# Loading each slab of left with two transfers of 64 x 8 pieces in place of four of 64 x 4

## The chip, the core and the metric

The kernel runs on one core of a Trainium2 chip. The metric is the device time of the whole program in microseconds (us), the median of several runs. Five engines matter: PE (matrix multiplies; PEld is its weight load), DVE, ACT and POOL (elementwise work) and SP, which does no arithmetic here and issues nearly all DMA transfers, one after the other, in the order of the program. SPq in the profile is SP's stream of such issues.

## What is computed

Two layers of the same form, one after the other, on x of 1 x 512 x 512 x 64 (f32). The reference, cut to what matters:

```python
for layer in (L0, L1):
    g = group_norm(x, groups=32)                      # over all rows and columns
    xn = layernorm(g, norm_scale, norm_bias)
    left  = (xn @ Wl + bl) * mask * sigmoid(xn @ Wlg + blg)
    right = (xn @ Wr + br) * mask * sigmoid(xn @ Wrg + brg)
    out = 0
    for dd in range(-4, 5):                           # a band of nine rows
        out += left[:, i + dd, i, None, :] * right[:, i + dd]
    out = layernorm(out) * sigmoid(xn @ Wog + bog)
    x = x + out @ Wo + bo
```

For each of 128 channels the band is a matrix of 512 x 512 that is zero but near its diagonal; it multiplies the rows of right.

## The kernel before

**Tiling.** The 512 rows are cut into 9 blocks of 64 rows that overlap (`row_blocks`), because one multiply takes a 64 x 64 piece of the band. The columns are taken in two halves at a time, one on partitions 0 to 63 and the other on 64 to 127; each half is cut into 4 chunks of 64 columns. A layer so has 36 chunks, and a chunk is one period of a schedule written out by hand as a table of steps (`FIRST`, lines 39 to 67, for the first layer, `SECOND`, lines 69 to 97, for the second). The loop of lines 1116 to 1119 walks through the table once a period and calls the step's function with a unit number (a unit is 8 columns of both halves, so a period has 8 units). Instructions go to each engine's queue in exactly this order.

**Tiles.** `z` is a unit's input (12 buffers), which POOL and DVE normalise and PE transposes into `ZT` and `zT`. PE multiplies these by the weights, ACT takes the sigmoid `sg`, and DVE writes right into `RO`. `A` holds the band of left for the block at hand: for each of 8 slabs h (16 channels), 8 pairs of channels, 64 columns of the band, on 64 partitions, and the same once more on the other 64 partitions. `mix` (line 710) multiplies a slab of `A` by `RO`, 64 multiplies for a slab, 8 slabs a chunk, and ACT or DVE copies the result back into `RO`. POOL and ACT then normalise `RO` into `on`, PE transposes `on`, DVE multiplies by the gate into `ZH`, PE multiplies by Wo, and DVE adds the old x, held in `XR` (6 buffers), which SP stores to `mid_x` in the first layer and to `out` in the second.

**Left.** Left is computed once a layer and written to `left_of` in DRAM in a spread form, in which a row of 2 x 64 f32 at the right offset is a row of the band (`spread_left`). `take_left` (line 696) reads slab h of block n from there into `A[:, h]`: four transfers, over the two halves of the partitions (e) and the two halves of the slab's channel pairs (k). Each moves 64 rows of 4 pieces of 512 B, 128 KB.

**When left is read.** After the copy of slab h in a block's last chunk, `on_copy` puts (next block, h) in the list `slabs` (line 1092). Each `load` step (`on_load`, line 967) first takes one entry from that list, issues its transfers with `take_left`, and then issues the two transfers of the next unit's `z`. So the eight slabs of the next block are read within about one period, one ahead of each pair of `z` transfers, on SP's one queue, between the `XR` transfers (`fetch`, line 866) and the stores (`stored`, line 899). For the first block of a layer the list is filled by line 938 in the same way. There are 9 blocks x 8 slabs x 2 layers = 144 slabs, and 576 transfers of left.

Of the kernel before, what the change touches and what calls it, by code (L numbers as in the profile page):

```python
# [20 lines left out]
WIN = 4  # L21
NEAR = 2 * WIN + 1
S = 64
# [4 lines left out]
HA = 16  # L28
# [129 lines left out]
def tile_two_banded_layers(  # L158
# [8 lines left out]
    H = layers[0]["Wl"].shape[1]  # L167
# [19 lines left out]
    span = 2 * (S + 2 * WIN)  # L187
    size = S * H // 2 * span
    left_of = dram.tile([2, size], F32, name="left_of")
# [86 lines left out]
    def strided(v: bass.AP, at: int, *dims) -> bass.AP:  # L276

        return bass.AP(tensor=v.tensor, offset=v.offset + at, ap=[list(d) for d in dims])
# [417 lines left out]
    def take_left(n: int, h: int):  # L696

        held[h] = n
        q = HA // 4
        for e in range(2):  # L700
            for k in range(2):
                en.sync.dma_start(
                    A[e * S : (e + 1) * S, h, k * q : (k + 1) * q].rearrange("p h i t -> p h (i t)"),
                    strided(
                        left_of, n % 2 * size + (h * HA // 2 + k * q) * span + 2 * WIN,
                        (H // 2 * span, S), (span, q), (1, 2 * S),
                    ),
                )

    def mix(c: int, h: int, b: str) -> tuple:  # L710

# [203 lines left out]
    def layer(src: bass.AP, dst: bass.AP, w: dict, stats: bool, then=None):  # L915
# [51 lines left out]
        def on_load(n, t, alt, b):  # L967
            if slabs:
                take_left(*slabs.pop(0))
            if t in units and t not in early:  # L970
                load(src, units[t])
# [106 lines left out]
        def on_band(n, t, alt, b):  # L1078
            if chunk(t):
                c, h = chunk(t)  # L1080
                while held.get(h) != c // per:
                    take_left(*slabs.pop(0))
                mixed[t] = mix(c, h, b)
# [141 lines left out]
    A = keep.tile([P, H // HA, HA // 2, S, 2], F32, name="A")  # L1225
# [63 lines left out]
```

## Time and profile before

| | |
|---|---|
| median of 3 runs | 4260.02 us (4246.09 to 4260.52) |
| the profiled execution's own span | 4279.5 us |
| busy: PE, DVE, POOL, ACT | 3741.4, 3681.0, 3584.7, 3320.3 us |
| transfers of left (`A<-left_of`) | 576 of 128 KB, all issued by SP |
| transfers of z, of XR, and stores | 1152 of 128 KB, 1152, 1152 (112 or 120 KB) |
| moved in all | 596.25 MB, mean 139 GB/s |

The profile is of a single execution, 19.5 us longer than the median. Durations and sums below are of that execution. In the timeline views a row has a start in us, a length in us (a merged row's length holds the small gaps in it), engine, line, operation, tiles and count, and in brackets the idle time before it with what ended it. In the view of stretches of time a row has the stretch, its length, the busy time of PE, PEld, DVE, ACT and POOL with counts, the granted clock of PE, the mean busy share of the 16 DMA engines, and GB/s. Nearly every instruction has line 491, which is the helper that records them, so they are told apart by tiles.

### The profile page before, as it was taken

To read this page: it belongs to the slowest core of one execution; us is meant where nothing else is said; L and a number is where in the kernel's file an instruction comes from. 1 tells how busy PE (TensorE), PEld (TensorE's weight loads), DVE (VectorE), ACT (ScalarE), POOL (GpSimd) and SP (SyncE) were. 2 spreads that over 40 slices of the span, in tenths; PEclk is the share of its full clock that TensorE was granted. 3 is DMA by queue.
4 is the path that set the end of the run, shared out by engine and by line. 5 is a ranking of instruction groups with operands and counts; after the bars stand their busy time and mean duration, and the time that the engine had idled before them with its cause. 6 is when DMAs were issued, how large, how long until landed. Compare 5 with 4: busy or idle time off the path is not lost.

```text
span 4279.5 us, 223070 instructions
## 1 busy us (share of the span) xinstructions
PE 3741.4 (87%) x94986; PEld 3208.3 (75%) x94986; DVE 3681.0 (86%) x9911; ACT 3320.3 (78%) x6372; POOL 3584.7 (84%) x4566
## 2 busy tenths in 40 slices
PE   0158999999999999999975889999999898989998
PEld 0057888888888888888864778787878787878786
DVE  8968888888888888888867889898989898989897
ACT  0047888888888888888863778888889788978887
POOL 2368999999999999999837789898989898989883
PEclk9989999999999999999997999999999999999999
DMA  9843545454545454545344354545454545444533
GB/s 396 321 102 96 150 112 152 117 147 114 152 115 151 116 152 117 153 115 155 104 119 114 98 141 120 145 120 148 121 147 119 146 116 145 123 142 122 149 105 96
DMA packets 695718, 596.25 MB, mean 139 GB/s; under 512 B 138310, under 2 KB 549990, under 8 KB 692420
## 3 DMA queue, kind: packets, MB, share of 16 engines
q1 hardware_dynamic: 692212, 580.43, 47.6%
q8 instruction: 748, 12.26, 1.2%
q14 instruction: 246, 2.02, 0.2%
q0 software_dynamic: 2512, 1.56, 0.1%
HBM read 436.71 MB, written 149.74 MB: 137 GB/s over the span
## 4 chain that ended last, share of the span: by engine, by line
PE 77%; issue 4%; POOL 3%; DVE 3%; SPq 2%; DMA 2%; ACT 2%; POOLq 0%; DVEq 0%; ACTq 0%
PE banks L491 59%; PE bank L491 14%; PE acc L491 4%; POOL z L491 3%; SPq L491 2%; DMA z<-mid_x 1%; POOL on L491 1%; DVE ZH L491 1%; DVE sto L491 1%; DVE RO L491 1%; ACT RO L491 0%; DVE z L491 0%; ACT on L491 0%; DVE XR L491 0%; ACT sg L491 0%
## 5 line engine op out<-in xcount | busy, mean ns | idle before, releaser
L491 ACT ACTIVATE on<-RO,nm,rs 128x128 f32<-128x128 f32 x2484 | 1144.3, 499 | 176.0 <-PE banks L491 150.4
L491 POOL TENSOR_SCALAR on<-RO,rs,nm 128x128 f32<-128x128 f32 x2124 | 958.6, 463 | 354.7 <-PE banks L491 308.4
L491 PE MATMUL banks<-pack,ZT 64*128 64x128 f32 x9216 | 1000.4, 287 | 28.5 <-DVE RO L491 13.9
L491 PE MATMUL banks<-pack,zT 64*128 64x128 f32 x9216 | 947.0, 277 | 3.7 <-issue 3.7
L491 DVE TENSOR_TENSOR RO<-banks,sg 128x512 f32<-128x512 f32 x1152 | 778.3, 684 | 181.9 <-ACT sg L491 158.6
L491 PEld LDWEIGHTS banks<-pack,ZT 64*128 64x128 f32 x9216 | 765.2, 191 | 152.9 <-ACT zT L491 35.6
L491 DVE BATCH_NORM_STATS2 sto<-RO 128x6 f32<-128x256 f32 x2304 | 852.5, 412 | 3.0 <-ACT RO L491 3.0
L491 DVE SCALAR_TENSOR_TENSOR ZH<-banks,pack,ZH 128x896 f32<-128x896 f32 (+1 forms) x576 | 667.4, 1159 | 198.2 <-PE banks L491 153.4
L491 ACT ACTIVATE sg<-banks 128x512 f32<-128x512 f32 x1170 | 691.6, 595 | 171.7 <-PE banks L491 133.0
L491 POOL TENSOR_TENSOR z<-z,ga 128x512 f32<-128x512 f32 x556 | 719.2, 1294 | 111.3 <-DMA z<-mid_x 91.0
L491 PE MATMUL banks<-RO,A 64*64 64x64 f32 x36864 | 699.4, 223 | 122.7 <-issue 117.5
L491 PEld LDWEIGHTS banks<-RO,A 64*64 64x64 f32 x36864 | 623.3, 136 | 222.8 <-issue 160.3
L491 PEld LDWEIGHTS banks<-pack,zT 64*128 64x128 f32 x9216 | 747.9, 192 | 5.0 <-issue 4.1
L491 POOL TENSOR_TENSOR z<-z,gb 128x512 f32<-128x512 f32 x556 | 717.8, 1291 | 3.5
L491 PE MATMUL bank<-pack,ZH 128*64 128x64 f32 x18432 | 666.3, 226 | 21.1 <-DVE ZH L491 11.2
L491 PEld LDWEIGHTS bank<-pack,ZH 128*64 128x64 f32 x18432 | 593.2, 139 | 111.3 <-issue 56.0
L491 ACT COPY RO<-banks 128x1024 f32<-128x1024 f32 x540 | 542.8, 1011 | 163.3 <-PE banks L491 154.1
L491 POOL TENSOR_TENSOR z<-z,rs 128x512 f32<-128x512 f32 x586 | 617.2, 1060 | 50.7 <-DVE rs L491 48.7
L491 POOL TENSOR_TENSOR z<-z,sti 128x512 f32<-128x512 f32 x586 | 621.9, 1071 | 35.8 <-DVE sti L491 31.8
L491 ACT ACTIVATE ZH<-banks 128x896 f32<-128x896 f32 (+1 forms) x576 | 535.4, 929 | 83.1 <-PE bank L491 55.4
L491 PE MATMUL banks<-ZT,pack 64*128 64x448 f32 (+1 forms) x2304 | 573.3, 572 | 2.6 <-DVE ZH L491 1.4
L491 DVE BATCH_NORM_STATS2 sti<-z 128x6 f32<-128x128 f32 x2344 | 509.4, 282 | 63.8 <-POOL z L491 62.9
(202 smaller groups left out, 4053.8 us busy)
## 6 DMA issues: line engine op xcount, KB each, us to landing
z<-in_x_dram SPq DMA_DIRECT2D x576, 128.0 KB
A<-left_of SPq DMA_DIRECT2D x576, 128.0 KB
z<-mid_x SPq DMA_DIRECT2D x576, 128.0 KB
gn_x<-in_x_dram SPq DMA_DIRECT2D x16, 4096.0 KB
XR<-in_x_dram SPq DMA_DIRECT2D x448, 112.0 KB
mid_x<-XR SPq DMA_DIRECT2D x448, 112.0 KB
XR<-mid_x SPq DMA_DIRECT2D x448, 112.0 KB
out_dram<-XR SPq DMA_DIRECT2D x448, 112.0 KB
```

What stands on the lines that cost most here:

```text
L491: return lambda *a, **k: tc.keep_in_program_order(f(*a, **k))
```

## The change

`take_left` no longer halves a slab's channel pairs: the loop over k goes, and each of the two transfers left moves 64 rows of 8 pieces, 256 KB. The bytes, the tiles and the order of everything else stay.

```diff
         held[h] = n
-        q = HA // 4
+        q = HA // 2
         for e in range(2):
-            for k in range(2):
-                en.sync.dma_start(
-                    A[e * S : (e + 1) * S, h, k * q : (k + 1) * q].rearrange("p h i t -> p h (i t)"),
-                    strided(
-                        left_of, n % 2 * size + (h * HA // 2 + k * q) * span + 2 * WIN,
-                        (H // 2 * span, S), (span, q), (1, 2 * S),
-                    ),
-                )
+            en.sync.dma_start(
+                A[e * S : (e + 1) * S, h].rearrange("p h i t -> p h (i t)"),
+                strided(
+                    left_of, n % 2 * size + h * q * span + 2 * WIN,
+                    (H // 2 * span, S), (span, q), (1, 2 * S),
+                ),
+            )
```

On SP's queue, at the last chunk of a block in the second layer, where the slabs of the next block are read, this stands before the change (x4 means four such transfers in a row):

```order
L491 DMA out_dram<-XR_1084 56x512 x2
L491 DMA A<-left_of 64x4x128 x4
L491 DMA z<-mid_x 64x512 x2
L491 DMA XR_1088<-mid_x 56x512 x2
L491 DMA XR_1087<-mid_x 56x512 x2
L491 DMA A<-left_of 64x4x128 x4
L491 DMA z<-mid_x 64x512 x2
```

and this after it:

```order
L491 DMA out_dram<-XR_1084 56x512 x2
L491 DMA A<-left_of 64x8x128 x2
L491 DMA z<-mid_x 64x512 x2
L491 DMA XR_1088<-mid_x 56x512 x2
L491 DMA XR_1087<-mid_x 56x512 x2
L491 DMA A<-left_of 64x8x128 x2
L491 DMA z<-mid_x 64x512 x2
```

Nothing has changed its place; each group of four transfers of left, ahead of a pair of z transfers, has become a group of two. At the start of the second layer, where the first block's slabs are read right behind the transfer that saves left (`left_rows`), SP's queue had

```order
L491 DMA left_rows<-A 128x4608
L491 DMA A<-left_of 64x4x128 x4
L491 DMA z<-mid_x 64x512 x2
L491 DMA A<-left_of 64x4x128 x4
L491 DMA z<-mid_x 64x512 x2
```

and has now

```order
L491 DMA left_rows<-A 128x4608
L491 DMA A<-left_of 64x8x128 x2
L491 DMA z<-mid_x 64x512 x2
L491 DMA A<-left_of 64x8x128 x2
L491 DMA z<-mid_x 64x512 x2
```

The first layer starts in the same manner. On PE, DVE, ACT and POOL the instructions and their order are the same before and after; only PE's multiplies of a new slab wait for two transfers where they waited for four.

## The prediction

> **What bounds the kernel now.** I read the page first. It shows that no single engine is full, and that PE carries most of the chain that ended last:
>
> ```profile
> span 4279.5 us, 223070 instructions
> PE 3741.4 (87%) x94986; PEld 3208.3 (75%) x94986; DVE 3681.0 (86%) x9911; ACT 3320.3 (78%) x6372; POOL 3584.7 (84%) x4566
> PE 77%; issue 4%; POOL 3%; DVE 3%; SPq 2%; DMA 2%; ACT 2%; POOLq 0%; DVEq 0%; ACTq 0%
> ```
>
> SPq has 2% and DMA 2% of the chain, some 170 us together. A share of the whole says little, so the next view is by stage. A period begins with PE's first multiply of a chunk's first slab; this one begins at 2915.50, the next at 2973.38, so this period is 57.9 us long:
>
> ```profile
> 2915.50 0.29 PE L491 MATMUL banks<-RO,A 64*64 64x64 f32 x4
> 2973.38 0.33 PE L491 MATMUL banks<-RO,A 64*64 64x64 f32 x5
> ```
>
> It is the last chunk of a block in the second layer, in which the next block's eight slabs are read. The view of stretches has all eight such periods of that layer (one of them and the sum), and then eight ordinary periods (one, and the sum):
>
> ```profile
> 2915.50:2973.40 57.90, 52.42 (x1263) 44.36 (x1259) 47.47 (x126) 45.78 (x91) 48.44 (x61) 0.94 0.67 186
> sum 487.20, PE 419.53 PEld 358.91 DVE 380.01 ACT 367.32 POOL 387.55; mean PE 52.44 PEld 44.86 DVE 47.50 ACT 45.92 POOL 48.44
> ...
> 2863.70:2915.50 51.80, 49.03 (x1259) 41.86 (x1256) 47.22 (x126) 45.46 (x91) 48.44 (x61) 1.00 0.38 101
> sum 409.10, PE 389.94 PEld 334.07 DVE 377.93 ACT 364.28 POOL 387.52; mean PE 48.74 PEld 41.76 DVE 47.24 ACT 45.54 POOL 48.44
> ```
>
> A reading period takes 487.2 / 8 = 60.9 us, an ordinary one 409.1 / 8 = 51.1 us, with the same counts and the same busy time on POOL, DVE and ACT. **The eight periods are 78.1 us too long in all, 9.8 us each.** PE's extra 30 us of busy time there come with a granted clock of 0.94 in place of 1.00, so they look like a consequence of PE having stood still, not a cause. What does it wait for? The chain of that one period, and who waited for whom from 2484.7 to 4048.5 us (the whole stretch that holds the eight):
>
> ```profile
> by line: PE banks L491 48.0%; SPq L491 18.3%; PE bank L491 14.4%; DMA z<-mid_x 11.3%; POOL z L491 4.4%; issue 2.2%; POOL on L491 1.5%; POOLq L491 0.1%
> ...
> POOL z L491 <- DMA z<-mid_x: 70.3, 16, 7.7
> PE banks L491 <- POOL on L491: 52.5, 15, 7.6
> ...
> 2924.70 1.27 POOL L491 TENSOR_TENSOR z<-z,ga 128x512 f32<-128x512 f32 x1 [3.26 <-DMA z<-mid_x]
> 3387.36 1.26 POOL L491 TENSOR_TENSOR z<-z,ga 128x512 f32<-128x512 f32 x1 [7.72 <-DMA z<-mid_x]
> ```
>
> POOL waits 16 times, two times in each reading period, for a z that has not landed, 70.3 us in all; its normalisations (`on`) stand behind that in its queue, and PE waits for them. The z is late because it was issued late. SP's queue in that period:
>
> ```profile
> 2906.85 0.76 SPq L491 DMA_DIRECT2D out_dram<-XR  x2
> 2916.70 3.51 SPq L491 DMA_DIRECT2D A<-left_of  x4
> 2920.33 1.18 SPq L491 DMA_DIRECT2D z<-mid_x  x2
> ...
> 2932.71 2.63 SPq L491 DMA_DIRECT2D A<-left_of  x4
> ...
> 2946.24 3.16 SPq L491 DMA_DIRECT2D A<-left_of  x4
> 2949.51 1.19 SPq L491 DMA_DIRECT2D z<-mid_x  x2
> 2950.75 2.58 SPq L491 DMA_DIRECT2D A<-left_of  x4
> 2953.44 1.20 SPq L491 DMA_DIRECT2D z<-mid_x  x2
> 2954.68 3.25 SPq L491 DMA_DIRECT2D A<-left_of  x4
> 2958.03 1.19 SPq L491 DMA_DIRECT2D z<-mid_x  x2
> ...
> 2973.86 1.87 SPq L491 DMA_DIRECT2D XR<-mid_x  x4
> 2977.04 1.20 SPq L491 DMA_DIRECT2D out_dram<-XR  x3
> ```
>
> From 2907.6 to 2916.7 it stands still, since the first slab may not be overwritten before PE has used it for the last time (2915.50). From 2916.7 to 2975.7, 59 us, row follows on row: **the queue is full, and sets the pace of the period.** The DMA engines behind it are busy only 0.67 of the time.
>
> **The change part by part.**
>
> *Issues.* Each reading period loses 16 of 32 issues of left. The price of one before, and of the nearest shapes:
>
> ```profile
> L491 SPq DMA_DIRECT2D A<-left_of x576: 573/613/2137, 261.6 to 4039.1; - x192
> L491 SPq DMA_DIRECT2D left_of<-left_rows x64: 550/586/1846, 363.8 to 3966.3; - x64
> L491 SPq DMA_DIRECT2D XR<-in_x_dram x576: 315/429/1902, 327.8 to 2226.1; - x192
> L491 SPq DMA_DIRECT2D XR<-mid_x x576: 306/391/1773, 2370.9 to 4263.9; - x192
> ```
>
> The middle number is the median: 613 ns. Four in the row at 2932.71 take 2.63 us, 657 ns each with the gap. What an issue of 64 x 8 pieces costs no row shows. Below stands 573 ns, the least of the 64 x 4 form; above 2 x 613 = 1226 ns, if the price went by pieces. The other rows speak for the low end: XR in the first layer is 56 x 4 pieces and in the second 56 x 1, and costs 429 against 391, 38 ns for three more pieces a row; a transfer of left_rows has 16 x 64 = 1024 pieces and costs 586, less than one of left with 256. I take 0.66 us, 0.70 with the gap. A slab then takes 1.41 us of the queue in place of 2.63, **1.22 us less, 9.8 us in eight slabs**; at 1226 ns it would be 0.1 us, nothing.
>
> *DMA engines.* The same bytes are now asked for in half the time, and the engines may take over as the limit. Their pace when they are full shows where the layers begin (share 1.11 and 1.03):
>
> ```profile
> 270.00:282.00 12.00, 8.23 (x88) 7.85 (x88) 8.43 (x28) 4.79 (x9) 11.92 (x11) 0.64 1.11 209
> 2302.00:2308.00 6.00, 2.97 (x52) 2.67 (x48) 5.72 (x18) 3.14 (x7) 5.92 (x6) 0.98 1.03 238
> ```
>
> A slab is 524 KB: 2.51 us at 209 GB/s, 2.20 at 238. If the engines set the pace in every slab, it saves 0.12 to 0.43 us, 1.0 to 3.4 us a period, not 9.8. Over a whole period they are not the limit: 0.67 x 57.9 = 39 us of work stand against 59 - 9.8 = 49 us of queue, a share of 0.79. But slabs stand close together (three between 2946 and 2958), and there the queue asks for more than they give. I take **7.5 us a period**, nearer to the queue's 9.8, because of the 0.79.
>
> *Where the stalls go.* The lateness at the end of a period is 9.8 us; 7.5 of it goes and 2.3 stay, most of it at the first z, which has one slab ahead of it alone (2916.70 to 2920.33) and can gain little over 1 us of its 3.26. The engines are late next, then the first wait of SP for PE, which the change doesn't touch. Eight periods: 8 x 7.5 = **60 us**. POOL's stall is on PE's path one to one within the reading: 70.3 us waited, 78.1 us too long.
>
> *First layer.* Its eight reading periods, and eight others:
>
> ```profile
> sum 429.80, PE 413.12 PEld 360.51 DVE 371.17 ACT 365.86 POOL 397.29; mean PE 51.64 PEld 45.06 DVE 46.40 ACT 45.73 POOL 49.66
> ...
> sum 432.60, PE 412.89 PEld 360.20 DVE 371.34 ACT 366.27 POOL 396.91; mean PE 51.61 PEld 45.02 DVE 46.42 ACT 45.78 POOL 49.61
> ```
>
> They are no longer than the others (53.7 against 54.1 us), with PE at 51.6: PE hides SP's late issues there. Gain nothing, and if that cover were thin the gain would be positive too.
>
> *Starts of the layers.* Here the queue is full as well, but so are the engines (share 0.99), just behind the save of left:
>
> ```profile
> 262.00:295.00 33.00, 24.57 (x296) 23.02 (x294) 23.99 (x79) 16.97 (x32) 24.91 (x22) 0.70 0.99 242
> ```
>
> Between 0 and 7 slabs x 1.22 = 8.5 us for each; with full engines I take 1 us each, **2 us**.
>
> *PE.* Its multiplies of a slab wait for two transfers in place of four. The slab is used a period after it is asked for (first asked at 2916.70, first used at 2973.38), so a longer transfer costs nothing; that cover is some 50 us thick.
>
> Sum: 60 + 2 = 62 us less than the profiled 4279.5, that is 4217.5; the runs shown have a median 19.5 us lower, and the same 62 us off 4260.0 give **4198 us**.
>
> **A rule against it.** The row first: in the page's reading above, SP issues left at 657 ns for 131 KB, 200 GB/s, and the engines behind it have time left. The Trainium skill, "DMA: Bandwidth & Descriptors", section "Issuing engines are not separate DMA queues", holds that the time to initiate a transfer is usually small beside the transfer itself. By that rule the engines set the pace, and the change would bring the 1.0 to 3.4 us a period of the second rival alone. The share of 0.67 in a period full of issues speaks against the rule here; the shares of 1.03 to 1.11 at the layers' starts speak for it there.
>
> **The rivals.**
>
> *All of it goes* (chance 0.19). The engines keep up, the longer issues that now and then come in a row of four (3.51 and 3.22 beside 2.63) become fewer too, and a reading period becomes an ordinary one: 78 us, with 3 us at each start 84, 4176 us. For it: 0.79 is below 1. Against: the first z of each period stays behind a slab.
>
> *The engines take over* (0.13). Each slab moves at 209 to 238 GB/s; 8 x 1.0 to 8 x 3.4 = 8 to 27 us, 4252 to 4233 us. For it: the rates of the full stretches. Against: they were taken with the save of left in the same queue.
>
> *The change doesn't do what it says* (0.07). The price goes by pieces, 1226 ns for twice as many, and SP's queue stays as full: 4260 us. Against: 1024 pieces for 586 ns.
>
> *Slower* (0.03). A transfer of left that stands before engines with work waiting blocks SP, and with twice the bytes it blocks longer. Such blocking is in the trace, at the start of the second layer:
>
> ```profile
> 2295.42 4.96 SPq L491 DMA_DIRECT2D A<-left_of  x4
> ```
>
> Four issues take 4.96 us there, against 2.63. The place is each reading period of the second layer; the point from which it decides is a pair that takes over 2.63 us, so engines that give less than 524 / 2.63 = 199 GB/s to left. At 175 GB/s a pair takes 3.0 us, 0.37 more, times 64 slabs: 24 us, 4284. Against: the lowest rate of full engines is 209.
>
> **How the numbers follow.** The forecast itself has 0.58, between 4180 and 4220. The range reaches from the full relief, 4176, to inside the engines' case, 4240. A measurement of this kernel can tell about 0.5%, 21 us, from no change. Faster by more: 0.58 + 0.19 + 0.09 of the engines' 0.13 = 0.86; within: 0.07 + 0.04 = 0.11; slower: 0.03.
>
> **What would show it.** In the changed kernel's profile: 288 issues of left with a median near 0.65 us (over 1.2 would mean the rival of the price); SP's queue with gaps again before the end of a reading period; POOL's waits for z from the second layer down from 70.3 us to 20 or less, the second wait of each period gone and the first left; reading periods of 53 to 54 us; a DMA share there near 0.75, and near 1 if the engines took over; PE's clock at 1.00 in most of them; the first layer as it is. It would be wrong if z lands later behind the longer transfers than it was issued earlier, which would show as the same waits of POOL with earlier issues.

## The result, and the profile after

| | before | after |
|---|---|---|
| median (lowest to highest) | 4256.42 us (4246.09 to 4260.52), 4 runs | 4206.19 us (4204.93 to 4215.75), 4 runs |
| span of the profiled execution | 4279.5 us | 4214.0 us |

After divided by before is 0.9882, 95% interval 0.9865 to 0.9899: 1.2% faster, 50 us by the medians. The profiled execution of before is 23 us longer than its median, that of after 8 us, so the profiles differ by 65 us; what follows takes stages from the profiles and the whole from the timed runs. The changed kernel was timed twice more, on other chips: 0.9897 (0.988 to 0.9914) and 0.99 (0.9878 to 0.9923).

The page of the changed kernel: the busy times and the chain that ended last, in which SPq has gone from 2% to 0%.

```profile
PE 3733.6 (89%) x94986; PEld 3201.5 (76%) x94986; DVE 3679.0 (87%) x9911; ACT 3315.6 (79%) x6372; POOL 3576.5 (85%) x4566
...
PE 80%; DVE 6%; issue 5%; DMA 4%; POOL 4%; ACT 2%; SPq 0%; POOLq 0%; DVEq 0%; ACTq 0%
```

The view of one tile: the issues of left.

```profile
L491 SPq DMA_DIRECT2D A<-left_of x288: 599/612/2052, 261.8 to 3973.8; - x144
```

Half as many, at a median of 612 ns where the half-sized ones took 613: twice the pieces cost nothing at the issue.

SP's queue in the reading period that begins at 2894.7 us, the same chunk as the one shown of before:

```profile
2886.00 0.76 SPq L491 DMA_DIRECT2D out_dram<-XR  x2
2895.89 1.69 SPq L491 DMA_DIRECT2D A<-left_of  x2
2897.67 1.22 SPq L491 DMA_DIRECT2D z<-mid_x  x2
2898.95 1.86 SPq L491 DMA_DIRECT2D XR<-mid_x  x4
2900.90 1.99 SPq L491 DMA_DIRECT2D A<-left_of  x2
...
2922.45 1.28 SPq L491 DMA_DIRECT2D A<-left_of  x2
2923.84 1.21 SPq L491 DMA_DIRECT2D z<-mid_x  x2
2925.09 1.28 SPq L491 DMA_DIRECT2D A<-left_of  x2
...
2938.46 1.20 SPq L491 DMA_DIRECT2D z<-mid_x  x2
2940.41 1.15 SPq L491 DMA_DIRECT2D out_dram<-XR  x2
2943.31 1.09 SPq L491 DMA_DIRECT2D z<-mid_x  x2
```

The standstill ahead of the first slab is still there (2886.8 to 2895.9). The first two slabs take 1.69 and 1.99 us, the later ones about 1.3. Some 40 us behind the first slab gaps begin (the rows from 2938 on show two): the queue has caught up before the period ends. The stretches of the eight reading periods of the second layer (one of them, and the sum), and PE's and POOL's waits from 2483.5 to 3983.1 us, the stretch that holds all eight and the ordinary periods between them:

```profile
2894.70:2949.10 54.40, 50.63 (x1262) 42.73 (x1260) 47.20 (x126) 45.60 (x91) 48.30 (x61) 0.97 0.83 202
sum 429.60, PE 402.68 PEld 342.56 DVE 377.70 ACT 365.08 POOL 386.98; mean PE 50.34 PEld 42.82 DVE 47.21 ACT 45.63 POOL 48.37
```

```profile
PE banks L491 <- issue: 64.8, 67, 3.0
...
POOL z L491 <- DMA z<-mid_x: 23.4, 11, 2.9
...
PE banks L491 <- POOL on L491: 2.3, 5, 1.0
```

The sum of the eight fell from 487.2 to 429.6 us, 57.6 us. POOL's waits for z fell from 70.3 to 23.4 us, and PE's for POOL's normalisations from 52.5 to 2.3. The engines' share rose from 0.67 to 0.83 in the period shown; over the eight it is 0.83 to 0.90. A period is 53.7 us now, not the 51 us of an ordinary one. What PE waits for now is "issue", time in which the profile shows nothing that it waits for. These waits were there before as well; over the same stretch (2484.7 to 4048.5 us) the profile of before has

```profile
PE banks L491 <- issue: 59.9, 63, 1.8
```

Within the eight reading periods alone they rose from 1.9 to 3.0 us a period. That is 1.1 us more than in an ordinary period after the change (1.9 us). Another 1.4 us of the 2.7 is PE's busy time: 50.3 us against 48.9, with a granted clock between 0.91 and 1.00 where ordinary periods have 1.00.

In the first layer something went the other way. Its eight reading periods (the last of them, and the sum), and PE's idle rows in that last one:

```profile
1949.60:2008.60 59.00, 53.51 (x1380) 46.61 (x1376) 47.13 (x126) 46.33 (x88) 49.52 (x64) 0.97 0.83 180
sum 446.40, PE 417.93 PEld 364.75 DVE 372.24 ACT 365.96 POOL 396.15; mean PE 52.24 PEld 45.59 DVE 46.53 ACT 45.74 POOL 49.52
```

```profile
1963.85 1.83 PE L491 MATMUL banks<-RO,A 64*64 64x64 f32 x105 [1.89 <-issue]
1967.87 1.90 PE L491 MATMUL banks<-RO,A 64*64 64x64 f32 x109 [0.68 <-issue]
1973.15 0.29 PE L491 MATMUL banks<-pack,ZT 64*128 64x128 f32 x1 [2.46 <-issue]
```

They were 429.8 us in sum and are 446.4, 2 us more each. Before, the same chunk's three idle rows, in the profile of before:

```profile
1961.84 1.65 PE L491 MATMUL banks<-RO,A 64*64 64x64 f32 x90 [0.50 <-issue]
1965.85 1.67 PE L491 MATMUL banks<-RO,A 64*64 64x64 f32 x94 [0.62 <-issue]
1970.31 0.38 PE L491 MATMUL banks<-pack,ZT 64*128 64x128 f32 x2 [1.08 <-issue]
```

They are the same three places in PE's program, and each wait is longer: 2.2 us in sum became 5.0. So there were three questions: whether it is the number of issues that brought the gain; whether the first layer's loss is real; and what the waits for issue are.

### The profile page after: what moved, and what is told of

The parts are those of the page before. It is cut to its first block, busy times and chain, and to the rows that moved or that the text cites. A ratio compares the mean times of both kernels' runs of the same rounds, so it can differ in the third digit from the quotient of the medians.

```text
span 4214.0 us, 222743 instructions
## 1 busy us (share of the span) xinstructions
PE 3733.6 (89%) x94986; PEld 3201.5 (76%) x94986; DVE 3679.0 (87%) x9911; ACT 3315.6 (79%) x6372; POOL 3576.5 (85%) x4566
## 3 DMA queue, kind: packets, MB, share of 16 engines
q14 instruction: 243, 1.99, 0.2%
## 4 chain that ended last, share of the span: by engine, by line
PE 80%; DVE 6%; issue 5%; DMA 4%; POOL 4%; ACT 2%; SPq 0%; POOLq 0%; DVEq 0%; ACTq 0%
PE banks L491 61%; PE bank L491 15%; PE acc L491 4%; POOL z L491 3%; DVE gn_st L491 2%; DMA z<-mid_x 1%; DVE z L491 1%; DVE RO L491 1%; DVE ZH L491 1%; DVE sto L491 1%; POOL on L491 1%; DMA nb<-in_L_conv_norm_bias_dram 0%; DMA raw<-in_L_conv_Wrg_dram 0%; DMA brow<-in_L_conv_bl_dram 0%; DMA brow<-in_L_conv_br_dram 0%
```

## The experiments

Chips differ: the kernel before took 4285, 4272 and 4281 us on the three of this section. So times are compared as ratios to the kernel before on the same chip, or between kernels that ran side by side on one chip; the absolute times in the expectations start from the 4256 us of the first chip. Periods are from the start of PE's first multiply of a chunk to that of the next; "reading" is a block's last chunk, eight in each layer, and "others" are the 24 other periods behind the first reading one. PE's waits for issue are summed over the waits view of each period.

| run | of the kernel before (95%) | reading, layer 1 | reading, layer 2 | others, layer 2 |
|---|---|---|---|---|
| before | 1 | 53.7 us | 60.9 us | 51.3 us |
| after | 0.9882 (0.9865 to 0.9899) | 55.8 | 53.7 | 51.0 |
| e1, 7 + 1 pieces | 1.0009 (0.9997 to 1.002) | 54.1 | 61.0 | 51.5 |
| e2, second layer only | 0.9871 (0.9856 to 0.9886) | 53.4 | 54.0 | 51.3 |
| e3, first layer only | 1.002 (1.0008 to 1.0033) | 54.9 | 60.5 | 51.4 |
| e4, z first | 0.9889 (0.9874 to 0.9904) | 54.9 | 53.9 | 51.7 |
| e5, after again | 0.9897 (0.988 to 0.9914) | 55.2 | 54.2 | 51.4 |
| e6, second only, z first | 0.9872 (0.9853 to 0.9891) | 53.0 | 53.5 | 51.4 |
| e7, halves apart | 0.9909 (0.9889 to 0.9929) | 55.1 | 54.9 | 51.3 |
| e8, idle reads of 8 x 512 B | 1.0014 (1.0 to 1.0028) | 55.1 | 54.5 | 53.4 |
| e9, idle reads of 1 x 512 B | 0.9885 (0.9865 to 0.9905) | 54.9 | 54.3 | 51.2 |
| e10, idle reads of 2 x 2 KB | 1.0007 (0.9993 to 1.0021) | 55.6 | 54.1 | 53.1 |
| e11, second only again | 0.9884 (0.9867 to 0.9902) | 53.8 | 54.1 | 51.4 |
| e12, after again | 0.99 (0.9878 to 0.9923) | 55.6 | 54.1 | 51.2 |

### e1: as many issues as before, but most bytes in a long transfer

The edit, shortened, against the changed kernel:

```diff
-            en.sync.dma_start(... 8 pieces a row ...)
+            for k0, k1 in ((0, 7), (7, 8)):
+                en.sync.dma_start(... pieces k0 to k1 of a row ...)
```

> Each half of a slab again comes in two transfers, but of 7 and of 1 channel pairs: as many issues as before the change, the same bytes, and most of them in a long transfer. Theory 1 (the number of issues on SP's queue sets the reading periods of the second layer): the time of the kernel before, 4256 us, within 10; reading periods of the second layer 60 to 62 us, POOL's waits for z there 65 us or more. Theory 2 (the longer transfer itself is what helps, because it costs the engines or its completion less): near the changed kernel, 4206 to 4220 us, and reading periods of 53 to 56 us.

Measured: 4291.26 us against 4285.26 for the kernel before beside it, reading periods of the second layer 61.0 us. The eight reading periods, and POOL's wait, of this run:

```profile
sum 487.90, PE 416.06 PEld 354.47 DVE 379.92 ACT 367.04 POOL 386.41; mean PE 52.01 PEld 44.31 DVE 47.49 ACT 45.88 POOL 48.30
```

```profile
POOL z L491 <- DMA z<-mid_x: 73.6, 16, 6.7
```

This is the profile of before again: 487.9 us against 487.2, and 73.6 against 70.3. The same number of bytes in transfers of 224 and 32 KB brings nothing. **It is the number of issues that SP's queue has to make, not the length of a transfer,** that the second layer's gain comes from.

### e2, e3: the change in one layer alone

The edits, shortened:

```diff
-                take_left(*slabs.pop(0))
+                take_left(*slabs.pop(0), four if stats else two)      # e2
+                take_left(*slabs.pop(0), two if stats else four)      # e3
```

(`stats` is true in the first layer; "two" and "four" are the transfers a slab.)

> Two transfers of 64 x 8 a slab in the second layer, four of 64 x 4 in the first. In the profiles the reading periods of the first layer went from 53.7 to 55.8 us with the change, and PE's idle time put down to issue in them from 16.7 to 27.1 us. Theory A (the denser requests of left hold up PE's instruction stream, which the same DMA engines carry): the first layer is back at 53.7 us a reading period and the whole is 8 to 17 us faster than the changed kernel, 4190 to 4198 us. Theory B (the difference in the first layer is scatter between executions): as the changed kernel, 4203 to 4209 us.

> The other half: two transfers a slab in the first layer, four in the second. Theory A (denser requests cost PE its instructions, and the first layer has nothing to gain): 5 to 17 us slower than before the change, 4261 to 4273 us, with reading periods of the first layer of 55 to 56 us; those of the second stay at 60 to 62 us. Theory B (scatter): 4256 us within 4, first layer 53 to 54 us.

Measured: with the first layer alone changed the kernel is 0.2% slower than before, and the interval leaves out no change; its reading periods there are 54.9 us. With the second alone changed they are 53.4, and the time is 0.9871 of before. So the first layer's loss is real, by e3 some 9 us of the whole (3 to 14 by the interval). The reading periods carry it: 54.9 to 55.8 us in the nine profiles with two transfers there, 53.0 to 54.1 in the five with four. In these periods PE's waits for issue are 2.7 to 3.4 us with two transfers and 1.5 to 2.2 us with four. In e3 they are the whole difference, 3.3 us a period in place of 2.1. Its eight periods are 9.4 us longer in sum than those of before (429.80), and PE's busy time, 413.12 us before, is no longer:

```profile
sum 439.20, PE 412.35 PEld 360.11 DVE 371.64 ACT 365.50 POOL 396.19; mean PE 51.54 PEld 45.01 DVE 46.45 ACT 45.69 POOL 49.52
```

How much the whole gains by leaving the first layer as it was is less sure: see e11.

### e4: the z pair ahead of the slab

```diff
         def on_load(n, t, alt, b):
-            if slabs:
-                take_left(*slabs.pop(0))
             if t in units and t not in early:
                 load(src, units[t])
+            if slabs:
+                take_left(*slabs.pop(0))
```

> The changed kernel with the order in the load step turned round: the z pair is issued first, then the slab. Theory 1 says that what is left of POOL's waits for z in the second layer (23.4 us in the changed kernel's profile, most of it the first z of a reading period, behind SP's 9 us wait for PE and behind one slab) goes: waits for z under 6 us, reading periods of 51 to 52 us, in all 10 to 20 us faster than the changed kernel, 4186 to 4196 us. Rival (the engines, with a share of 0.86 in these periods, are now the bound, and PE's waits for issue make up the rest): the waits for z go, but the periods stay at 53 us or more and the time within 5 us of 4206.

Measured: 0.9889, and reading periods of 53.9 us in the second layer. The first expectation failed. No wait of POOL for z stands among the waits of that stretch any more. What stands there is this (waits of the run with z first, from its first to its last reading period):

```profile
PEld banks L491 <- issue: 110.9, 169, 2.8
...
PE banks L491 <- issue: 78.5, 70, 2.6
```

PE's waits for issue are 3.7 us a reading period here, in place of 3.0 in the changed kernel. A reading period is still 2.2 us longer than an ordinary one of this run (51.7), with no z late: what stays is not z's lateness.

### e5 to e7: after again, second layer only with z first, and a slab's halves apart

e5 is the changed kernel, e6 is e2 with the z pair ahead of the slab in both layers, and e7 puts one transfer of a slab at a load step and the other at the next fetch step (shortened):

```diff
-                slabs.append(((c + 1) // per, h))
+                slabs.extend((((c + 1) // per, h, 0), ((c + 1) // per, h, 1)))
...
         def on_fetch(n, t, alt, b):
+            if slabs:
+                take_left(*slabs.pop(0))
```

> The changed kernel once more, beside the next three on one chip. All theories: 0.986 to 0.990 of the kernel before. With it the second-layer-only kernel (0.9871 of the kernel before) is put in its place: theory A (denser requests cost the first layer PE's instructions) wants this one 0.1 to 0.3% slower than that, 0.988 to 0.990; scatter wants 0.987.

> Two transfers a slab in the second layer, four in the first, and in both the z pair ahead of the slab. The z-first kernel had no waits for z left and yet reading periods of 53.9 us, with PE's waits for issue at 3.7 us a period in place of 1.9. Theory A: the order brings nothing, so this is as the second-layer-only kernel, 0.986 to 0.989. Rival (the order helps the second layer and hurt the first, where the z-first kernel had 54.9 us reading periods): 0.982 to 0.985.

> The changed kernel with the two transfers of a slab no longer next to each other: one at a load step, one at the next fetch step of the table. Same issues, same sizes, same bytes, shorter bursts. Theory A (bursts of left hold up PE's instruction stream): PE's idle time put down to issue in the reading periods falls from 3.0 to 3.4 us a period towards 2.2, in both layers, and the whole is 5 to 15 us faster than the changed kernel run beside it. Rival (it is the total of requests in the period, not their spacing): issue waits stay at 3 us or more, time within 5 us.

Measured on one chip: 4227.08 us (4223.03 to 4232.83) for after, 4216.77 (4215.67 to 4217.82) for e6, 4231.17 (4224.29 to 4244.66) for e7. The runs of e6 all lie below those of after, by 10 us in the median, though the two intervals to the kernel before overlap. Its ratio, 0.9872, is that of e2 without the order turned round (0.9871), so the order earned nothing that can be seen. Shorter bursts (e7) brought nothing either: PE's waits for issue were 4.1 us a reading period in the second layer and 2.7 in the first, where theory A wanted 2.2. Spacing a slab's two transfers out in this way does not help; the total of a period may be what counts.

### e8 to e10: idle reads in ordinary periods

e8 is the changed kernel with reads that nothing waits for, in the periods of the second layer that read no slab:

```diff
             if slabs:
                 take_left(*slabs.pop(0))
+            elif not stats and 12 <= t < max(units):
+                for e in range(2):
+                    en.sync.dma_start(
+                        extra[e * S : (e + 1) * S],
+                        strided(
+                            mid_x, (e * S * L + t % NU * 8) * D,
+                            (L * D, S), (16 * D, HA // 2), (1, 2 * S),
+                        ),
+                    )
```

e9 reads one piece of 512 B a row in place of eight, e10 two pieces of 2 KB. None of the three leaves anything of the layer out.

> The changed kernel with idle reads added in the second layer: in the periods that read no slab, two transfers of 64 x 8 pieces of 512 B go ahead of each z pair, from mid_x into a tile that nothing reads. Each ordinary period then asks for as many bytes as a reading one, with nothing waiting for them. Theory A: PE's waits for issue in these 27 periods rise from 1.9 to about 3 us, DMA share to about 0.85, and the periods from 51.0 to 52.5 to 54 us, 40 to 80 us in all. Rival (the 53.7 us of the reading periods come from something that only the slabs do, such as the first wait of SP for PE): the ordinary periods stay at 51 to 51.5 us.

> The kernel with idle reads, with as many of them (two at each load step of the ordinary periods of the second layer) but one piece of 512 B a row in place of eight: SP issues as much, the DMA engines carry an eighth. Theory A (what costs PE is work on the DMA engines): ordinary periods back at 51.4 to 51.8 us, PE's issue waits at 2.3 us, the whole within 0.3% of the changed kernel. Rival (the longer queue of issues on SP is what costs): 53 us or more, as with the full reads.

> The idle reads at full size, 256 KB each, but as two pieces of 2 KB a row in place of eight of 512 B. If the bytes alone count: as with the eight pieces, ordinary periods of 53.4 us, PE's issue waits of 3.2 us, DMA share near that run's. If the number of pieces counts: the share falls and the periods stand between, 51.8 to 52.8 us.

Measured: e8 took 4279.76 us, 52.7 more than after beside it, and gave back the whole gain. e9, with as many issues and an eighth of the bytes, is 0.9885 of before, like after, so SP's longer queue is not the cause. e10, with all the bytes in a quarter of the pieces, is nearly like e8 (53.1 and 53.4 us). The view of stretches has the ordinary periods in threes, from one reading period to the next; the seventh three of after (e5), then of e8, e9, e10, each from its own run:

```profile
3788.50:3942.90 154.40, 146.92 (x3772) 125.28 (x3769) 142.48 (x376) 137.73 (x269) 145.41 (x181) 1.00 0.40 115
```

```profile
3829.80:3990.90 161.10, 149.58 (x3770) 127.37 (x3768) 142.44 (x376) 137.55 (x269) 145.24 (x181) 0.98 0.76 189
```

```profile
3788.80:3941.80 153.00, 147.18 (x3773) 125.21 (x3771) 142.33 (x376) 137.59 (x269) 144.99 (x181) 1.00 0.45 128
```

```profile
3832.30:3991.80 159.50, 149.10 (x3775) 126.98 (x3771) 142.63 (x376) 137.75 (x269) 145.00 (x181) 0.99 0.68 186
```

The length goes with GB/s: 115 and 128 GB/s give 154 and 153 us, 189 and 186 give 161 and 160. And PE's waits in these stretches, of after (e5) and of e8:

```profile
PE banks L491 <- issue: 7.5, 7, 1.5
```

```profile
PE banks L491 <- issue: 11.5, 8, 3.0
```

Nearly as often, and the waits are longer. Over the 24 such periods, PE's waits for issue are 2.3 us a period in e5, 3.2 in e8, 2.0 in e9 and 3.4 in e10. So **traffic on the DMA engines alone, with nothing of the kernel waiting for it, lengthens PE's waits for issue and the period**, which grows by 2.0 us in e8. The waits are 0.9 us of this. The other 1.1 us is PE's busy time, 50.05 us a period in place of 48.98, at a mean granted clock of 0.97 in place of 1.00; why the clock fell is open.

What are these waits? PE's own program arrives by DMA. Among the queues, the page before counts

```profile
q8 instruction: 748, 12.26, 1.2%
```

These are packets of 16 KB. PE's record in that trace, weight loads and sequencer included, has 191525 instructions, 256 to a packet. The Trainium skill, "Runtime: NRT & Kernel Launch", section "Instruction fetch mechanics", says that an engine's instructions are refilled in blocks of 16 KB by a DMA queue of its own and that this is mostly hidden; the size agrees with the trace, and "mostly hidden" holds for eight of the eleven packets in each of the two first-layer periods shown above, not for the three behind which PE waits 2.2 us before and 5.0 after.

That the waits are for these packets is shown by their places, counted in PE's record. The three waits of that period come behind 86722, 86978 and 87233 of its instructions, in both profiles: a packet's worth apart. Of PE's 150 waits for issue above 0.3 us in the profile of before, 145 stand at one place of a block of 256 (behind 193 or 194 of its instructions), and of its 106 other waits of that length, 4. The packets' times say the same: in that period three packets end at 1960.36, 1964.36 and 1968.99 us before, at 1962.20, 1966.50 and 1971.66 after, and 1.3 to 1.7 us behind each of them PE goes on.

What denser traffic changes is when a packet begins. From PE's start at that place of a block to the start of the next packet, 1.0 to 1.1 us pass on average in the first layer's reading periods of the five profiles with four transfers, 1.4 to 1.6 us in the nine with two; in the ordinary periods of the second layer it is 0.8 us in e5 and 0.9 in e9, but 1.2 in e8 and in e10. The packet itself is hardly longer: in the first layer's reading periods 1112 ns on average before, 1183 after, and 1174 in e2, which has four transfers there. What holds a packet back ahead of its start, the traces do not show.

### e11, e12: second layer only beside after

> Two transfers a slab in the second layer, four in the first, now beside the changed kernel on one chip. Theory A: 0.1 to 0.3% (4 to 13 us) faster than the changed kernel in the same call, with reading periods of the first layer at 53 to 53.7 us against 55 to 56. Scatter: the two within 3 us.

> The changed kernel beside the run before this one: 0.988 to 0.990 of the kernel before; reading periods of the first layer 55 to 56 us, of the second 53.5 to 54.5.

Measured: 4231.02 us (4222.12 to 4234.62) against 4233.43 (4221.95 to 4249.0). Reading periods of the first layer are 53.8 against 55.6 us, close to what theory A expected, but the whole differs by 2.4 us, which these runs can't tell from nothing. The loss in the first layer's reading periods, 14.3 us in sum, is partly given back by the other periods of that layer (53.4 us each in e11, 53.2 in e12, 5 us in sum). Less of the slabs' reading runs over into those: in e11 the last issue of left comes up to 4.7 us behind the end of a reading period, in e12 3.5 to 6.7 us ahead of it.

## Why the prediction was right, and where it was off

The predicted 4198 us and 62 us of gain stand against 4206 us and 50 us; the range held it.

- **The bound.** SP's full queue in the second layer's reading periods was the right reading. e1 shows it: the old number of issues, whatever their length, brings back the old time.
- **The price of an issue.** 0.66 us was taken, between 0.573 and 1.226; it is 0.612. The rows with many pieces had pointed the right way. Most slabs take 1.3 us of the queue, not 1.41. The queue was relieved of more than the 9.8 us of the sum: the eight slabs of the period shown take 11.4 us in place of 23.9.
- **The second layer's periods.** 60 us were predicted, from 60.9 to 53 to 54 us a period; they gained 57.6 and stand at 53.7. The number was right for a partly wrong reason. What stays was put down to the first z of the period and to late data. POOL does still wait for z (23.4 us in all), but e4 takes the wait away and the period stays: PE's waits for issue take its place. That the sum came out so near is luck: the queue lost more than was reckoned, and PE's waits and its lower clock took part of it back.
- **The engines.** They were feared as the next bound, by way of z landing late. A share near 0.75 was forecast; it is 0.86 on average. The sum took the engines' work in a period as fixed, some 39 us. It is 39.6 us before and 46.2 after, for the same 8192 pieces of 512 B of left: a piece takes 33 ns on average before and 41 after. In e1, whose long transfers come at the old pace, it takes 34, which points to the density of the traffic, not to the transfer's length. But z was not what the engines delayed most. The clock of 1.00 in most reading periods did not come either: it is 1.00 in three of the eight, 0.91 to 0.97 in the others. The "rule against it" led to 1.0 to 3.4 us a period, with the engines setting the pace; 7.2 us came. e1 and after carry the same bytes, and the number of issues decides: issues follow one another on SP.
- **The first layer.** "Gain nothing, and if that cover were thin the gain would be positive too" was wrong in sign, and it is the step that failed. It looked only at who waits for SP. With PE at 51.6 of 53.7 us, the layer had nothing to gain from an earlier z, and something to lose from denser traffic, which brings PE's instructions later: 1 to 2 us a reading period, and 0.2% of the whole by e3, 8.6 us at 4285. Put in place of the zero, 57.6 - 8.6 leaves 49 us, near the 50 measured; the 57.6 are from profiles and the 8.6 from timed runs of another chip, so the closeness proves little.
- **The starts of the layers.** 2 us were predicted. First multiplies of a slab stand at 299.7 us before and 299.9 after in the first layer; the stretch from the first layer's last chunk (2161.3 and 2165.5) to the second's first (2331.5 and 2336.4) is 170.2 and 170.9 us. No gain; this fits the row with share 0.99, by which the engines were full there.
- **The rivals.** That all of it goes fell by the same waits for issue and the lower clock; that the engines take over fell by the 7.2 us a period; that the price goes by pieces and that SP would block longer fell by the 612 ns and the 1.3 us.

Not explained: the ordinary periods and the first three of the second layer are some 13 us shorter in the profile of after than in that of before. The profiled execution of before was itself a long one, and the first three periods come to between 145.6 and 152.0 us in the other runs without idle reads, with either number of transfers, so this is taken as scatter between executions.

No version here beats the change beyond doubt. Two transfers in the second layer, four in the first, with z first, was 10 us faster beside it on one chip; without z first it was 2.4 us faster on another.

## What to carry to other kernels

Where one queue issues all transfers, add up its rows in the stage that is too long: if they follow on each other without gaps, the number of issues is the cost, and where an issue of twice the size costs no more (612 against 613 ns here), half as many save half of it. Then ask who else uses the DMA engines in the stages that have nothing to gain: there, the same bytes in less time can slow the engine that is the bound, whose instructions come over the same engines. A stretch filled with reads that nobody waits for measures that price by itself.

## What the runs showed that was not expected

The price of an issue of left went with neither bytes nor pieces: medians of 613 ns for 64 x 4 pieces, 612 for 64 x 8, and in e1 605 for 64 x 7 and 626 for 64 x 1. Idle reads of some 4 MB in a period of 51 us made it 2.0 us longer (e8), though the engines' share was only 0.76 and nothing waited for the data. And PE's waits for issue stand 256 instructions apart, at the places where it needs the next packet of its own program.
